# The experts' gate and up products by Strassen's scheme, in a kernel of two transformer layers

## The chip, the cores and the metric

The kernel runs on one core of a Trainium2 chip. The core has TensorE (PE, matrix products; its weight loads are listed apart as PEld), VectorE (DVE), ScalarE (ACT), GpSimd (POOL) and SyncE (SP), which work side by side and wait for each other by semaphores. POOL also issues the indirect DMAs, which gather or scatter rows by an index. The metric is the device time of the whole program in microseconds (us). Seventeen runs of the kernel before gave a median of 1565.16 us, between 1560.81 and 1569.68.

## The reference

Two layers work on 2 x 2048 tokens of width 256, in float32. The part that matters here is the end of the second layer, a mixture of eight experts of which each token takes two. Cut to that, it reads:

```
xf = x.reshape(B * T, D)                       # 4096 x 256
pi = sinkhorn(-(xf @ gate_W.T))                # 4096 x 8
_, top_idx = top_k(pi, 2)
g = einsum('nd,efd->enf', xf, W_gate)          # f: 1024 hidden units
u = einsum('nd,efd->enf', xf, W_up)
y = einsum('enf,edf->end', silu(g) * u, W_down)
out = sum over k of y[top_idx[:, k], n] * pi[:, k]
```

Before it come a gated linear attention with a quantised feed-forward product (layer 0) and an attention of 16 heads with linear biases (layer 1). The change leaves them alone.

## The kernel before

The program has three stages in time: layer 0, the attention of layer 1 (with the routing of the experts beside it), and the experts, which begin at about 840 us of the profiled execution.

The routing sorts the 8192 pairs of token and expert into 32 **blocks** of 256 rows, each with one expert, and two **groups** of four small remainders. `Experts.pieces` (line 2478) goes over the blocks; what it does for one is in `Block`:

- `load` (line 2234) issues two gathers on POOL, `load_gate_up` with 2 MB of gate and up weights and `load_down` with 1 MB of down weights (both line 2209), and on SP the load of the block's rows of the table (`load_places`, line 2225). They are issued at the start of block n for block n + 2.
- `fetch_rows` (line 2239) makes, on DVE, the list of row numbers `to` and the weights `wt` (lines 2244 to 2251), and gathers the 256 rows of normalised tokens into `xb` by two indirect DMAs on POOL (line 2464). It runs in the middle of block n for block n + 2.
- `open_rows` (line 2256) transposes the rows by four products with the identity on PE (line 2265), and ACT copies the 128 x 512 result out of PSUM (line 2270). It runs at the end of block n for block n + 1.
- `hidden` (line 2272) makes the 1024 hidden units in eight slices of 128. A slice has four products of 128 x 128 weights with 256 columns (line 2279): gate and up, each summed over the two halves of the width 256. ACT then takes the silu of the gate (line 2284) and DVE multiplies it by the up product (line 2285). The slices take turns in several PSUM banks.
- `add_rows` (line 2289) multiplies the hidden units of the block before with its down weights: 16 products of 256 columns (line 2308), after the hidden products of the present block. `send` (line 2313) scales the 128 x 256 results on DVE (line 2315) and adds them to the rows of the output by an indirect DMA on POOL (line 2318), one for each of the two tiles of rows. The second one writes to the same tensor as the first, and it is issued only when the first has landed.

A float32 product shows as two records in the profile, each with its own weight load. So the 1024 gate and up products of 32 blocks are 2048 records, and the 512 down products are 1024.

The steps of the two groups (`Group`, from line 2325) are put between blocks: 12 gathers of weights, a gather of rows and four scatters for each group, with their products.

The order on an engine is set in two ways. A framework places each instruction when, by its own plan, its inputs are ready, in the order in which the program names them where several are ready. An instruction that goes through `keep_in_program_order`, or through the small class `InOrder` (line 110) that does this for each call, is put behind the instruction that the program names before it on that engine, whichever that is. At run time each engine works its list strictly in order: an instruction that waits holds back all behind it. In the kernel before, the products, silus and multiplications of the experts are placed freely; the transposes and the small DVE steps of `fetch_rows` are pinned.

The buffers of the experts stage are borrowed from the attention by `rooms` (line 1884): three rooms of gate and up weights, four of down weights, two each for the turned rows and the hidden units. PSUM has six banks for products (tag `mm`) and two for the down products.

Of the kernel before, what the change touches and what calls it, by code (L numbers as in the profile page):

```python
# [1683 lines left out]
def attention(  # L1684
# [198 lines left out]

    def rooms(name, n, shape, dt=F32):
# [12 lines left out]
        if name == "wdown" and n % 4 < 2:  # L1897
            return operands.heads[2][:, n % 4, :]
        if name in ("hT", "wdown"):
            n = n % 2 + (2 if name == "wdown" else 0)  # L1900
            if n not in larger:
                larger[n] = p2.tile([P, 4 * ST], F32, tag="pt", name="larger", bufs=4)
            return larger[n] if n >= 2 else larger[n].rearrange("p (f r) -> p f r", f=NFC)
        if name == "xT":
            t = operands.first_values.rearrange("p t d -> p (t d)")
            return t[:, n % 2 * ST : (n % 2 + 1) * ST].rearrange("p (e r) -> p e r", e=2)
        if name == "sg":
            if name not in larger:
                larger[name] = p2.tile([P, 4, BS], F32, tag="sk_beaten", name="sg", bufs=1)
            return larger[name][:, n % 4, :]  # L1910
        if name == "y":
            t = other_values.rearrange("p t d -> p (t d)")
            return t[:, n % 4 * NC * E : (n % 4 + 1) * NC * E].rearrange("p (c d) -> p c d", c=NC)
# [10 lines left out]
    for n, (pieces, widths, masks, ended) in enumerate(units):  # L1924
# [22 lines left out]
        if routed:  # L1947
            next(sends, None)
            next(decision, None)
        else:  # L1950
            routed = next(background, True) is True
        if n == len(units) - 4:
            ahead[0].open_rows()
# [244 lines left out]
class Block:  # L2198


    def __init__(self, e, n, b):
        self.e, self.n, self.b = e, n, b
        self.tiles, self.rows, self.first = NC, BS, b * BS

# [29 lines left out]
    def load(self):  # L2234
        self.load_gate_up()
        self.load_down()
        self.load_places()
# [17 lines left out]

    def open_rows(self):


        nc, rooms, n, keep = (
            self.e.nc, self.e.rooms, self.tiles, self.e.tc.keep_in_program_order  # L2260
        )
        ps = rooms("x_ps", self.n, [P, 2 * BS]).rearrange("p (e r) -> p e r", e=2)
        for e in range(2):
            for c in range(n):
                keep(nc.tensor.transpose(  # L2265
                    ps[:, e, c * P : (c + 1) * P], self.xb[:, c, e * P : (e + 1) * P],
                    self.e.c.ident,
                ))
        self.xT = rooms("xT", self.n, [P, 2, BS])
        nc.scalar.copy(self.xT[:, :, 0 : self.rows], ps[:, :, 0 : self.rows])  # L2270

    def hidden(self):
        nc, rooms, rows = self.e.nc, self.e.rooms, slice(0, self.rows)
        self.hT = rooms("hT", self.n, [P, NFC, BS])
        for f in range(NFC):
            ps = rooms("h_ps", f, [P, 2 * BS]).rearrange("p (j r) -> p j r", j=2)
            for j in range(2):
                for c in range(2):
                    nc.tensor.matmul(  # L2279
                        ps[:, j, rows], lhsT=self.wgu[:, j, c, f * P : (f + 1) * P],  # L2280
                        rhs=self.xT[:, c, rows], start=c == 0, stop=c == 1,
                    )
            sg = rooms("sg", f, [P, BS])[:, rows]
            nc.scalar.activation(sg, ps[:, 0, rows], AF.Silu)  # L2284
            nc.vector.tensor_tensor(self.hT[:, f, rows], sg, ps[:, 1, rows], ALU.mult)  # L2285
            if f % 2:
                yield

    def add_rows(self, apart=False):

# [4 lines left out]
        else:  # L2295
            ps = self.e.rooms("y_ps", self.n, [P, NC * E]).rearrange("p (c d) -> p c d", c=NC)
            parts = [ps[:, c, :] for c in tiles]
        for c in tiles:
            self.multiply(c, parts[c])
            if apart:  # L2300
                self.send(c, parts[c], y)
        if not apart:
            for c in tiles:
                self.send(c, parts[c], y)

    def multiply(self, c, ps):
        for fc in range(NFC):
            self.e.nc.tensor.matmul(  # L2308
                ps, lhsT=self.hT[:, fc, c * P : (c + 1) * P], rhs=self.wd[:, fc, :],
                start=fc == 0, stop=fc == NFC - 1,  # L2310
# [136 lines left out]
class Experts:  # L2447
# [3 lines left out]
    def __init__(self, tc, a, out, c, rooms, blocks, groups):  # L2451
        self.tc, self.nc, self.a, self.out, self.c = tc, tc.nc, a, out, c
        self.rooms = rooms
# [24 lines left out]
    def pieces(self, begun=False):  # L2478
# [5 lines left out]
        if todo and not begun:  # L2484
            for block in todo[0:2]:
                block.load()
                block.fetch_rows()
            todo[0].open_rows()
        for n, block in enumerate(todo):
# [3 lines left out]
            for part, _ in enumerate(block.hidden()):  # L2493
                if last and part == 0:
                    todo[n - 1].add_rows()
                if part == 1 and n + 2 < len(todo):
                    todo[n + 2].fetch_rows()
                yield
            if not last:
                todo[n + 1].open_rows()  # L2500
            if n and not last:
                todo[n - 1].add_rows()
# [3 lines left out]
        if todo:  # L2506
            todo[-1].add_rows(apart=True)
# [4 lines left out]
def layer1_experts(tc, a, out, c, blocks, groups):  # L2512
    bufs = {"wgateup": 3, "wdown": 4, "xb": 4, "y": 4, "at": 5, "by": 5, "wt": 5, "to": 5,
# [180 lines left out]
```

## Time and profile before

| | |
|---|---|
| median of 17 runs | 1565.16 us |
| the profiled execution | 1564.67 us |
| its span, first to last instruction | 1562.8 us |
| PE busy / PEld busy | 1509.5 us (97%) / 1222.9 us (78%) |
| DVE / ACT / POOL busy | 710.7 (45%) / 641.5 (41%) / 452.0 (29%) us |
| gate and up products, line 2279 | 2048 records, 449.1 us busy |
| down products, line 2308 | 1024 records, 226.6 us busy |
| mean granted clock of TensorE | 0.989 of full speed |

The page gives busy time by engine, the span in 40 slices, the chain of work that ended last, and the costliest groups of instructions by line. Each group has its operands, partitions x elements, the number of records, the busy time and the mean length of one in ns, and the idle time before them with what ended it. The length of a matmul record holds the time that its result needs to come out of the array, so records of a dense row overlap: what one costs is the distance from its start to the next start. The timeline gives starts and lengths, the windows give the busy time of each engine in a stretch, with the granted clock.

### The profile page before, as it was taken

The numbers are of one execution on the slowest core, as the hardware profiler recorded it, in microseconds if no ns is written. First come the engines' busy times: TensorE is split into PE (matmuls) and PEld (weight loads), VectorE is DVE, ScalarE is ACT, GpSimd is POOL, SyncE is SP. The second block draws the span as 40 slices with busy tenths as digits, with TensorE's granted clock in tenths as the row PEclk, the third lists the DMA queues.
The fourth block names the chain that finished last, engine by engine and source line by source line (L and its number), as shares of the span: only waits on it lengthen the run. The fifth ranks groups of instructions, "written<-read, shape, count | busy, mean of one in ns | idle before, by whom it ended". The sixth has DMA issues, their size and how long they took to land.

```text
span 1562.8 us, 32176 instructions
## 1 busy us (share of the span) xinstructions
PE 1509.5 (97%) x13412; PEld 1222.9 (78%) x13412; DVE 710.7 (45%) x2223; ACT 641.5 (41%) x1336; POOL 452.0 (29%) x385
## 2 busy tenths in 40 slices
PE   7889999999999999999999999999999999999996
PEld 4556766766678888788888888888888888888885
DVE  6787767655378876844445222122222221222121
ACT  4444546455467777677774211111111111111110
POOL 4342222112010000771101333333334433343232
PEclk9989999999999999999999999999999999999998
DMA  7001102311460210602305765575856768576521
GB/s 221 0 21 50 56 28 70 75 56 56 118 120 17 46 45 29 105 20 67 114 16 197 224 184 188 181 245 165 286 178 200 221 195 283 166 229 198 184 31 22
DMA packets 75562, 191.59 MB, mean 123 GB/s; under 512 B 18976, under 2 KB 56352, under 8 KB 62944
## 3 DMA queue, kind: packets, MB, share of 16 engines
q0 software_dynamic: 28256, 144.23, 29.2%
q1 hardware_dynamic: 46048, 44.04, 11.3%
q8 instruction: 107, 1.75, 0.5%
q10 hardware_dynamic: 1104, 1.18, 0.2%
q14 instruction: 47, 0.39, 0.1%
HBM read 157.95 MB, written 31.83 MB: 121 GB/s over the span
## 4 chain that ended last, share of the span: by engine, by line
PE 64%; DVE 1%; DMA 0%; issue 0%; POOL 0%; POOLq 0%
PE h_ps L2279 28%; PE y_ps L2308 14%; PE sc L1828 9%; PE o_ps L1848 7%; PE f_ps L1538 1%; PE o_tr L1784 1%; PE x_ps L2265 1%; PE h_ps L2390 1%; PE on_tr L1803 0%; PE h_ps L2425 0%; DVE pt L118 0%; DMA out<-va,to 0%; PE h_ps L2308 0%; PE h_ps L2413 0%; POOL out L2318 0%
## 5 line engine op out<-in xcount | busy, mean ns | idle before, releaser
L2279 PE MATMUL h_ps<-va,qk 128*128 128x256 f32 x2048 | 449.1, 380 | 0.0
L2279 PEld LDWEIGHTS h_ps<-va,qk 128*128 128x128 f32 x2048 | 387.9, 190 | 57.3 <-issue 4.8
L1834 ACT ACTIVATE pt<-sc 128x512 f32<-128x512 f32 (+1 forms) x589 | 302.8, 601 | 103.0 <-ACT pt L1834 42.2
L2284 ACT ACTIVATE sg<-h_ps 128x256 f32<-128x256 f32 x256 | 98.1, 383 | 531.0 <-PE h_ps L2279 531.0
L2285 DVE TENSOR_TENSOR larger<-sg,h_ps 128x256 f32<-128x256 f32 x256 | 107.9, 422 | 329.2 <-ACT sg L2284 329.1
L1828 PE MATMUL sc<-qk 32*128 32x256 f32 (+6 forms) x3544 | 207.6, 333 | 3.4 <-issue 1.5
L1828 PEld LDWEIGHTS sc<-qk 32*128 32x128 f32 x3544 | 176.6, 186 | 32.7 <-issue 17.8
L1848 PE MATMUL o_ps<-pt,va 128*32 128x256 f32 (+7 forms) x3544 | 162.7, 312 | 1.2 <-DVE o_sb L118 1.1
L2318 POOL DMA_INDIRECT out<-va,to x64 | 101.9, 1592 | 172.2 <-issue 73.6
L1848 PEld LDWEIGHTS o_ps<-pt,va 128*32 128x32 f32 x3544 | 126.4, 110 | 26.5 <-issue 6.9
L118 DVE TENSOR_TENSOR pt<-pt,keepmask 128x128 f32<-128x128 f32 (+3 forms) x568 | 121.0, 273 | 36.3 <-ACT pt L1834 35.8
L2177 POOL DMA_INDIRECT table<-rows,place x64 | 63.9, 998 | 200.5 <-DVE pt L118 181.3
L2315 DVE SCALAR_TENSOR_TENSOR va<-y_ps,wt,half_bias 128x256 f32<-128x256 f32 x63 | 27.6, 480 | 203.0 <-PE y_ps L2308 203.0
L2308 PE MATMUL y_ps<-qk,larger 128*128 128x256 f32 x512 | 113.3, 379 | 0.0
L2308 PE MATMUL y_ps<-larger 128*128 128x256 f32 x496 | 109.7, 379 | 0.0
L2308 PEld LDWEIGHTS y_ps<-qk,larger 128*128 128x128 f32 x512 | 96.0, 190 | 12.3
L2308 PEld LDWEIGHTS y_ps<-larger 128*128 128x128 f32 x496 | 93.2, 190 | 12.1
L2464 POOL DMA_INDIRECT xb<-normed,to x64 | 63.6, 994 | 38.6 <-issue 16.8
L2209 POOL DMA_INDIRECT qk<-in_wgateup,wrow x32 | 30.1, 942 | 99.8 <-PE h_ps L2279 55.2
L532 PE MATMUL vf_ps<-qk,xnT 128*128 128x512 f32 x128 | 58.5, 611 | 0.0
L2209 POOL DMA_INDIRECT qk<-in_wdown,wrow x16 | 15.1, 943 | 147.2 <-PE y_ps L2308 72.5
L532 PEld LDWEIGHTS vf_ps<-qk,xnT 128*128 128x128 f32 x128 | 24.3, 195 | 29.1 <-issue 25.6
(281 smaller groups left out, 1791.2 us busy)
## 6 DMA issues: line engine op xcount, KB each, us to landing
qk<-qk SPq DMA_DIRECT2D x32, 256.0 KB
qk<-qk SPq DMA_DIRECT2D x64, 128.0 KB
va<-v SPq DMA_DIRECT2D x4, 1208.0 KB
v<-v SPq DMA_DIRECT2D x8, 574.0 KB
normed<-xn SPq DMA_DIRECT2D x8, 512.0 KB
out<-acc SPq DMA_DIRECT2D x8, 512.0 KB
acc<-in_x SPq DMA_DIRECT2D x7, 512.0 KB
table<-rows,place POOLq DMA_INDIRECT x64, 4.4
```

Source lines behind the costliest of these rows:

```text
L118: return lambda *a, **k: self.tc.keep_in_program_order(begin(*a, **k))
L532: tc.keep_in_program_order(nc.tensor.matmul(*args, **kwargs))
L1828: nc.tensor.matmul(scs[r][:, at : at + q1 - q0], lhsT=heads[rows, 1, kb * P : (kb + 1) * P], rhs=heads[rows, 0, qt * QT + q0 : qt * QT + q ...
L1834: nc.scalar.activation(pt[:, r, 0:width], scs[r][:, 0:width], AF.Exp)
L1848: nc.tensor.matmul(sums[bank][r * HR : (r + 1) * HR, to + q0 : to + q1], lhsT=values[b, way][:, kb, h * VC : h * VC + HR], rhs=pt[:, r, at ...
L2177: send = self.nc.gpsimd.indirect_dma_start(out=self.c.table, in_=self.rows[:, t, :], in_offset=None, out_offset=bass.IndirectOffsetOnAxis( ...
L2279: nc.tensor.matmul(ps[:, j, rows], lhsT=self.wgu[:, j, c, f * P : (f + 1) * P], rhs=self.xT[:, c, rows], start=c == 0, stop=c == 1,)
L2284: nc.scalar.activation(sg, ps[:, 0, rows], AF.Silu)
L2285: nc.vector.tensor_tensor(self.hT[:, f, rows], sg, ps[:, 1, rows], ALU.mult)
L2308: self.e.nc.tensor.matmul(ps, lhsT=self.hT[:, fc, c * P : (c + 1) * P], rhs=self.wd[:, fc, :], start=fc == 0, stop=fc == NFC - 1,)
L2318: nc.gpsimd.indirect_dma_start(out=self.e.out, in_=y[:, c, :], in_offset=None, out_offset=bass.IndirectOffsetOnAxis(ap=self.to[:, c : c + ...
L2464: self.nc.gpsimd.indirect_dma_start(out=to, out_offset=None, in_=self.c.normed, in_offset=bass.IndirectOffsetOnAxis(ap=at, axis=0),)
```

## The change

The gate product G = X Wg and the up product U = X Wu of a block are read as one product of 2 x 2 blocks: the rows of X in two tiles of 128, the width 256 in two halves, and the weights in gate and up. Eight products of such blocks become seven, by Strassen's scheme in Winograd's form, on sums and differences of the operands.

- **`combine`** is new. For half u of the hidden units (512 of them) it makes four sums or differences of weights, each 128 x 512: two on POOL (`s1`, and the room of `up[0]` overwritten) and two on DVE (`s2`, `s4`), all pinned. It is named after each half of block n for the same half of block n + 1, and for block 0 six units before the end of the attention and at the start of the stage.
- **`open_rows`** gets three subtractions on DVE behind the copy, pinned, and moves from the end of block n to the middle of its second half.
- **`hidden`** has, for each half, seven products P1 to P7 of four slices with 128 columns. P1 is copied out of its PSUM tile `w` by ACT, P6 and P7 are added into the same tile and copied out again, P4 is added last and read by DVE. P2 goes to tile `z`, P5 and P3 to tile `v`. DVE adds and multiplies 128 x 512 tiles, ACT takes two silus. Everything is pinned on its engine.
- **`add_rows`** is now a generator of eight pieces of two down products. `hidden` calls four of them in each half: one after P2, one after P5 and two after P7. The eighth piece is followed by the two `send`s.
- **`load_down`** moves from the start of block n to its end (still for block n + 2), with three rooms for down weights in place of four. The `y` rooms go from four to two. Other rooms are laid out anew.

```diff
+        if n == len(units) - 6:
+            ahead[0].combine(0)
         if n == len(units) - 4:
             ahead[0].open_rows()
...
     def load(self):
         self.load_gate_up()
-        self.load_down()
         self.load_places()
...
+    def combine(self, u):
+        e, (gate, up) = self.e, (
+            [self.wgu[:, j, c, u * ST : (u + 1) * ST] for c in range(2)] for j in range(2)
+        )
+        s1, s2, s4 = (e.rooms("combo", 3 * u + n, [P, ST]) for n in range(3))
+        e.gpsimd.tensor_tensor(s1, up[0], up[1], ALU.add)
+        e.gpsimd.tensor_tensor(up[0], gate[0], up[0], ALU.subtract)
+        e.vector.tensor_tensor(s2, s1, gate[0], ALU.subtract)
+        e.vector.tensor_tensor(s4, gate[1], s2, ALU.subtract)
+        self.factors[u] = (gate[0], gate[1], s4, up[1], s1, s2, up[0])
+
     def open_rows(self):
...
+        for i, (k, c) in enumerate(((0, 0), (0, 1), (1, 1), (1, 0))):
+            e.tensor.transpose(ps[:, i, :], self.xb[:, c, k * P : (k + 1) * P], e.c.ident)
+        x = e.rooms("xT", self.n, [P, 4, P])
+        e.scalar.copy(x, ps)
+        t, s = (e.rooms("xt", 2 * self.n + i, [P, 2, P]) for i in range(2))
+        vector.tensor_tensor(t, x[:, 1:3, :], x[:, 0:2, :], ALU.subtract)
+        vector.tensor_tensor(s[:, 0, :], x[:, 2, :], t[:, 0, :], ALU.subtract)
+        vector.tensor_tensor(s[:, 1, :], x[:, 3, :], s[:, 0, :], ALU.subtract)
...
+            def product(n, ps, first=False, last=False):
+                for f in range(4):
+                    e.tensor.matmul(
+                        ps[:, f, :], lhsT=self.factors[u][n - 1][:, f * P : (f + 1) * P],
+                        rhs=self.turned[n - 1], start=first and f == 0, stop=last and f == 3, skip_group_check=True,
                     )
...
+            sg = e.rooms("sg", u, [P, 2, 4, P])
+            one, two = (self.hT[:, 4 * u : 4 * u + 4, c * P : (c + 1) * P] for c in range(2))
+            product(1, w, first=True)
+            e.scalar.copy(sg[:, 0], w)
+            product(2, z, first=True, last=True)
+            e.vector.tensor_tensor(sg[:, 0], sg[:, 0], z, ALU.add)
+            next(others, None)
+            product(6, w)
+            e.scalar.copy(sg[:, 1], w)
+            e.scalar.activation(sg[:, 0], sg[:, 0], AF.Silu)
+            product(5, v, first=True)
+            next(others, None)
+            product(7, w)
+            e.scalar.copy(two, w)
+            e.vector.tensor_tensor(two, two, v, ALU.add)
+            yield
+            next(others, None)
+            next(others, None)
+            product(4, w, last=True)
+            e.vector.tensor_tensor(one, sg[:, 0], w, ALU.mult)
+            product(3, v, last=True)
+            e.vector.tensor_tensor(sg[:, 1], sg[:, 1], v, ALU.add)
+            e.scalar.activation(sg[:, 1], sg[:, 1], AF.Silu)
+            e.vector.tensor_tensor(two, two, sg[:, 1], ALU.mult)
+            yield
...
+        for half in range(2):
+            for c in tiles:
+                for n in (4 * half, 4 * half + 2):
+                    self.multiply(c, parts[c], range(n, n + 2), c == 0, c > 0)
+                    if n < NFC - 2 or c < NC - 1:
+                        yield
         for c in tiles:
-            self.multiply(c, parts[c])
...
+            self.send(c, parts[c], y)
+        yield
...
+        self.tensor, self.vector, self.scalar, self.gpsimd = (
+            InOrder(tc, engine) for engine in (self.nc.tensor, self.nc.vector, self.nc.scalar, self.nc.gpsimd)
+        )
...
         for n, block in enumerate(todo):
             if n + 2 < len(todo):
                 todo[n + 2].load()
             last = n + 1 == len(todo)
-            for part, _ in enumerate(block.hidden()):
-                if last and part == 0:
-                    todo[n - 1].add_rows()
+            others = todo[n - 1].add_rows() if n else iter(())
+            for part, _ in enumerate(block.hidden(others)):
                 if part == 1 and n + 2 < len(todo):
                     todo[n + 2].fetch_rows()
+                if part % 2 and not last:
+                    todo[n + 1].combine(part // 2)
+                if part == 2 and not last:
+                    todo[n + 1].open_rows()
                 yield
-            if not last:
-                todo[n + 1].open_rows()
-            if n and not last:
-                todo[n - 1].add_rows()
+            if n + 2 < len(todo):
+                todo[n + 2].load_down()
             while between and between[0][0] <= n and not last:
                 between.popleft()[1]()
```

## The prediction

> **What bounds the kernel now.** I began with the page. PE is busy almost throughout, and the chain that ended last is PE's own, led by the line that the change replaces.
>
> ```profile
> PE 1509.5 (97%) x13412; PEld 1222.9 (78%) x13412; DVE 710.7 (45%) x2223; ACT 641.5 (41%) x1336; POOL 452.0 (29%) x385
> ...
> L2279 PE MATMUL h_ps<-va,qk 128*128 128x256 f32 x2048 | 449.1, 380 | 0.0
> ```
>
> Then the windows of the experts stage (columns: window, length, busy us and records of PE, PEld, DVE, ACT and POOL, granted clock, DMA share, GB/s). PE has no gap; the others are a quarter to a third busy. While this holds, PE's records are the time.
>
> ```profile
> 900.00:1180.00 280.00, 280.00 (x1356) 241.70 (x1355) 61.49 (x177) 48.95 (x120) 99.43 (x86) 1.00 0.63 201
> ```
>
> Next the timeline of PE, for the distance from one record to the next (columns: start, length, engine, line, tiles, count). 13 records of 256 columns last 2.97 us; less the last one's 0.379, over 12, that is 0.216 us each. 16 records of 128 columns with 128 x 128 weights, in layer 0, last 1.95; less 0.275, over 15, 0.1117 us. Half the columns cost 0.52, not 0.50.
>
> ```profile
> 1060.72 2.97 PE L2279 MATMUL h_ps<-va,qk 128*128 128x256 f32 x13
> ```
> ```profile
> 24.09 1.95 PE L532 MATMUL c_ps<-qk,soft 128*128 128x128 f32 x16
> ```
>
> Last POOL's timeline. The gather of down weights waits for PE's last down product, so its starts give the period of a block: 1078.65 - 1057.49 = 21.16 us. The second scatter (L2318) starts 5.95 us after the first.
>
> ```profile
> 1057.49 0.94 POOL L2209 DMA_INDIRECT qk<-in_wdown,wrow  x1 [6.40 <-PE y_ps L2308]
> 1058.74 1.61 POOL L2318 DMA_INDIRECT out<-va,to  x1 [0.30 <-issue]
> 1064.69 1.58 POOL L2318 DMA_INDIRECT out<-va,to  x1 [4.34 <-issue]
> 1066.58 1.01 POOL L2464 DMA_INDIRECT xb<-normed,to  x1 [0.30 <-issue]
> 1067.89 0.99 POOL L2464 DMA_INDIRECT xb<-normed,to  x1 [0.30 <-issue]
> ...
> 1078.65 0.94 POOL L2209 DMA_INDIRECT qk<-in_wdown,wrow  x1 [6.41 <-PE y_ps L2308]
> ```
> ```profile
> 1523.21 1.56 POOL L2318 DMA_INDIRECT out<-va,to  x1 [11.28 <-DVE va L2315]
> 1527.75 1.55 POOL L2318 DMA_INDIRECT out<-va,to  x1 [2.97 <-DMA out<-va,to]
> ```
>
> With no gather of weights just ahead it is 4.54 us: issue 1.56, landing 2.97.
>
> **PE's own work.** A block has 64 records of gate and up, 32 of down (0.216 each: 13.81 + 6.91) and 4 transposes of 0.11 (0.44): 21.16, the period seen. After, 2 halves x 7 products x 4 slices x 2 = 112 records of 0.1117 are 12.51; with down and transposes 19.86. That is 1.30 less per block, 41.6 over 32.
>
> The Trainium skill, "TensorE: Matmul & The Clock Gate", section "The mechanism", speaks against the change: a weight load overlaps running matmuls only in other row groups, and by "LDWEIGHTS" it takes columns / 1.2 GHz, 107 ns. By that estimate, load and product one after the other, the 3584 records would cost about 0.214 each and the change 325 us. The row of 128 columns above contradicts it.
>
> **The new waits.** All is now pinned on its engine, and two chains run beside PE. Their prices are rows of the same size:
>
> ```profile
> L118 DVE TENSOR_TENSOR acc<-acc,f_ps 128x512 f32<-128x512 f32 x32 | 22.0, 687 | 26.7 <-PE f_ps L1538 25.9 <-PE sk_ps L1538 0.8
> L2315 DVE SCALAR_TENSOR_TENSOR va<-y_ps,wt,half_bias 128x256 f32<-128x256 f32 x63 | 27.6, 480 | 203.0 <-PE y_ps L2308 203.0
> L219 POOL TENSOR_TENSOR mx_r<-mx_r,mx_pw 128x512 f32<-128x512 f32 x17 | 21.6, 1272 | 83.9 <-DVE mx_r L218 57.7 <-DVE arg L719 23.6 <-DVE ln_veo L144 2.5
> L2270 ACT COPY va<-x_ps 128x512 f32<-128x512 f32 x32 | 18.8, 586 | 4.5 <-PE x_ps L2265 2.9
> L1834 ACT ACTIVATE pt<-sc 128x512 f32<-128x512 f32 x579 | 299.3, 604 | 98.2 <-ACT pt L1834 41.0 <-issue 30.8 <-PE sc L1828 24.7
> ```
>
> So a large DVE step is 0.69 (0.69 from SBUF alone too, L201), a POOL sum 1.27, a copy 0.59, a silu 0.60 (Exp's row), a product of P1 to P7 0.89, a piece 0.86. A result leaves PE 0.2 after its last slot; a hand-off between other engines takes 0.03 to 0.08, taken as 0.05.
>
> P4 adds into `w`, so it waits for the copy of P7. ACT makes that copy behind the first silu, which waits for DVE's addition of P2. DVE makes that behind `s4` and `s2` of the `combine` named before it, and `s2` waits for POOL's `s1`. So PE's P4 hangs on POOL.
>
> Chain A, from P4 of a block's first half to P4 of its second: P4 and P3 1.79, out of PE 0.2, `sg1` addition 0.69, silu 0.60, multiplication 0.69, `to` 0.17 (L2244), two gathers of `xb` 2.6 (`s1` is pinned behind them), `s1` 1.27, `s2` and `s4` 1.38, addition 0.69, silu 0.60, copy 0.59, six hand-offs 0.3: 11.6 us. PE's work in the same stretch is seven products, four pieces, the transposes: 10.15. PE waits 1.4.
>
> Chain B, from there to P4 of the next block's first half. The eighth piece ends as P4 starts, but its `send` is behind the opened rows on DVE: copy 0.59, three subtractions 1.01 (L118 rows of 256 and 128 columns: 0.43, 0.29, 0.29), `send` 0.48, first scatter to second 4.54, second scatter and its gap 1.88, `s1` 1.27 (pinned behind it), `s2` and `s4` 1.38, addition 0.69, silu 0.60, copy 0.59, hand-offs 0.3: 13.3 us. PE's work is seven products and four pieces, 9.71. It waits 3.6, part of it at P6, whose copy is behind the previous silu on ACT.
>
> The period is 24.9 us where it was 21.16. Thirty blocks have both chains.
>
> **The price of `s2` beside POOL.** `up[0]` runs on POOL as `s1` ends, beside `s2` and `s4`. Bounds: 0 (DVE's 0.69 unchanged) and 1.27 (the whole of it) per chain. In the nearest row, a DVE step with two SBUF inputs began 0.20 us after a POOL step and took 1419 ns, not 693:
>
> ```profile
> L210 DVE SCALAR_TENSOR_TENSOR mx_r<-mx_pw,mx_v x16: 658/693/1419, 34.7 to 356.1; 128x512 f32<-128x512 f32 x16
> ```
>
> I take its 0.73, twice per block: period 26.3, or 5.2 more than before; 30 x 5.2 = 156.
>
> **The clock.** Where PE was busy 1.31 of 3.42 us (a gap of 2.57 in it), the granted clock was 0.50 in the next window:
>
> ```profile
> 97.13:100.55 3.42, 1.31 (x12) 1.12 (x11) 3.42 (x12) 0.79 (x2) 2.35 (x1) 1.00 0.00 0
> 100.55:103.96 3.41, 2.95 (x8) 2.12 (x9) 2.88 (x11) 1.10 (x3) 1.11 (x2) 0.50 0.00 0
> ```
>
> The wait before P4 is of that size, once per block. Half clock for 3.4 us costs PE 1.7, of which only P4 and P3 are on chain A: 0 to 1.8 per block. I take 1.0, as the rest falls into PE's spare time: 30.
>
> The Trainium skill, "TensorE: Matmul & The Clock Gate", section "Why this matters for your kernels", allows gaps of up to about 3 us; by it this term would be nearer 0. The row's gap of 2.57 already halved the clock.
>
> **The rest.** The groups' POOL work (24 gathers of 1.25, eight scatters of 4.5) now delays sums, while 25 us of their products (L2390, L2425, L2413, L2377) fill PE's waits: between 0 and 30, taken as 10, since their gathers fit into POOL's free time and only the scatters exceed it. Block 0 has no pieces to cover its copies, and the last has no sums to wait for: -3 to 8, taken as 3. `combine` for block 0 in the attention: nothing, as POOL idles there for 67 us (768 to 836) and its weights were asked for at 739; without that cover 4 us once. `load_down` later: nothing, since its weights are used two blocks on; one period if that failed. SP's table load stays where it was, and nothing new is queued behind it. PSUM: three tiles per half in six banks, read long before their turn comes again: nothing, or 0.7 per half if a bank were late. DVE (11 us of work per block) and ACT (6.6) are not bounds.
>
> **The sum.** 1564.67 + 156 (in which PE's saving is included) + 30 + 10 + 3 = 1763.7 us against the profiled execution, whose time is 0.5 below the median.
>
> **Rivals.** (1) The chains hide, and PE stays the bound: 1564.67 - 41.6 = 1523. For it: PE has no gap now, and DVE and ACT would be at most 55% busy. It decides if the two chains together take less than 21.16, 5.2 less than I have; the wait for the first scatter (4.5) and the gathers ahead of `s1` (2.6) would have to fall out. Against it: the scatter's wait stands in the trace before.
> (2) The scatters don't hold `s1` (the order on POOL turns out otherwise), chain A alone binds: 11.6 + 9.7 + 0.7 = 22.0, 1564.67 + 30 x 0.84 + 13 = 1603 at most, 1569 without the price beside POOL and the 13 of the rest.
> (3) A weight load costs its recorded 190 ns, not its distance: 3584 x 0.190 = 681 in place of 442, 1804. Against: 16 records in 1.95 us.
> (4) All bounds at their upper end, with a weight gather ahead of the first scatter (5.95, not 4.54): 5.2 + 1.1 + 1.8 + 1.4 = 9.5 per block, 1564.67 + 285 + 38 = 1888.
>
> **Chances.** The two chains, 1603 to 1825: 70%. Rival 1: 10%. Rival 2: 11%, of which 2% within 0.2%, about what a measurement here can tell from no change. Rivals 3 and 4, 9% together, half below 1825. The range reaches from 1600 to 1825 and leaves out about 2 in 10: rival 1, most of rival 2, the upper end of rival 4. So faster 10%, same 2%, slower 88%.
>
> **What would show it.** Right: L2279's successor at 0.112 per record, PE with two waits per block, the longer before P4 of the first half, released by ACT; `s2` released by POOL, POOL's sums right behind the second scatter; a period near 26; the clock at 0.5 in places. Wrong: PE busy 100% with a period of 19.9, or `s1` ahead of the scatters on POOL. The weakest steps are the price beside POOL, the clock, and the order of POOL's list, which I take from the pins in the code.

## The result and the profile after

The changed kernel takes 1763.58 us (median of 8 runs, 1762.21 to 1766.29) where the kernel before takes 1564.87 (47 runs): a ratio of 1.1276, 95% interval 1.1264 to 1.1289. It is 199 us slower, and 1763.7 was forecast. The profiled execution has a span of 1759.2 us.

First the page of the kernel after. Every operation that is now pinned on its engine is recorded at line 118, so the groups are told apart by their tiles.

```profile
PE 1537.7 (87%) x14948; PEld 1282.9 (73%) x14948; DVE 994.8 (57%) x2511; ACT 721.8 (41%) x1400; POOL 646.8 (37%) x513
...
L118 PE MATMUL h_ps<-va,qk 128*128 128x128 f32 x1024 | 149.4, 300 | 75.1 <-ACT larger L118 75.0
```

PE's busy share fell from 97% to 87%, and the groups of gate and up products, which had no idle time ahead of them before, now wait for ACT. The same window of the experts stage as before (length, then busy us and records of PE, PEld, DVE, ACT and POOL, granted clock, DMA share, GB/s) says how much:

```profile
900.00:1180.00 280.00, 230.13 (x1563) 206.94 (x1563) 137.97 (x233) 64.26 (x115) 140.06 (x108) 0.93 0.49 155
```

PE rests for 50 of 280 us where it rested for none, at a mean granted clock of 0.93 in place of 1.00. DVE and POOL, the next, are busy for half of it: no engine is the bound by its own work. Such a picture calls for the waits, here those of the kernel after by engine (who waited for whom: us in total, times, longest):

```profile
ACT larger L118 <- DVE larger L118: 263.8, 55, 12.3
...
PE h_ps L118 <- ACT larger L118: 156.0, 51, 9.8
DVE larger L118 <- POOL larger L118: 121.7, 26, 11.7
DVE va L118 <- POOL va L118: 102.7, 26, 10.3
...
POOL out L2376 <- DMA out<-va,to: 34.3, 17, 3.8
```

Read from the second line outwards, this is the chain of the prediction: PE's P4 waits for ACT's copy, ACT's silu for DVE's addition, DVE's `s2` for POOL's `s1`, and POOL, ahead of `s1`, for the landing of the first scatter. DVE's two waits for POOL go by tile: `va` holds the first half's sums, `larger` the second half's. PE's timeline shows one such wait (start, length, engine, line, tiles, count, idle time before):

```profile
1046.07 2.07 PE L118 MATMUL h_ps<-second,qk 128*128 128x128 f32 x8 [3.65 <-ACT larger L118]
1047.94 1.92 PE L118 MATMUL h_ps<-larger,bidx 128*128 128x128 f32 x8
...
1060.04 1.16 PE L118 MATMUL h_ps<-second,qk 128*128 128x128 f32 x8 [0.64 <-ACT larger L118]
1061.03 1.06 PE L118 MATMUL h_ps<-larger 128*128 128x128 f32 x8
...
1075.74 1.95 PE L118 MATMUL h_ps<-va,qk 128*128 128x128 f32 x16
```

At 1046.07 P4 of a first half has waited 3.65 us, and it and P3 then take 2.07 and 1.92 us where the second half's take 1.16 and 1.06: the clock is halved just where it counts. The last line is the pace at full clock: 16 records in 1.95 us less one record's own tail, 0.112 us each, as in layer 0 before.

POOL's timeline has the order on which the chain hangs:

```profile
1030.48 0.96 POOL L2229 DMA_INDIRECT larger<-in_wdown,wrow  x1 [0.76 <-PE y_ps L118]
1034.39 1.63 POOL L2376 DMA_INDIRECT out<-va,to  x1 [2.95 <-DVE va L2373]
1036.32 0.98 POOL L2229 DMA_INDIRECT qk<-in_wgateup,wrow  x1 [0.30 <-PE h_ps L118]
1039.00 1.59 POOL L2376 DMA_INDIRECT out<-va,to  x1 [1.70 <-DMA out<-va,to]
1040.05 1.85 POOL L118 TENSOR_TENSOR larger<-qk 128x512 f32<-128x512 f32 x1
1041.97 1.77 POOL L118 TENSOR_TENSOR qk<-qk 128x512 f32<-128x512 f32 x1
...
1055.93 1.78 POOL L118 TENSOR_TENSOR qk<-qk 128x512 f32<-128x512 f32 x1
...
1294.39 1.59 POOL L2494 DMA_INDIRECT out<-group_y,group_to  x1 [2.24 <-DMA out<-va,to]
...
1298.40 1.59 POOL L2494 DMA_INDIRECT out<-group_y,group_to  x1 [0.73 <-DMA out<-group_y,group_to]
...
1305.68 1.63 POOL L2494 DMA_INDIRECT out<-group_y,group_to  x1 [0.30 <-issue]
...
1311.17 1.59 POOL L2494 DMA_INDIRECT out<-group_y,group_to  x1 [1.43 <-DMA out<-group_y,group_to]
...
1316.72 1.60 POOL L2376 DMA_INDIRECT out<-va,to  x1 [2.68 <-DMA out<-group_y,group_to]
```

The second scatter waits for the first (4.61 us from start to start), and `s1` and `up[0]` stand directly behind it. In two blocks the four scatters of a group stand on POOL's list too, 4.0 to 7.3 us from one to the next, and three of the five waits shown end with the landing of a group's scatter; those blocks last 36.6 and 37.6 us. The other 28 between the first block and the last have a mean period of 27.36 us.

DVE's timeline beside POOL's step at 1055.93 shows the price of two engines side by side: `s2` takes 0.69 us, and `s4` 1.64.

```profile
1055.88 0.69 DVE L118 TENSOR_TENSOR va<-va,qk 128x512 f32<-128x512 f32 x1 [3.56 <-POOL va L118]
1056.61 1.64 DVE L118 TENSOR_TENSOR bidx<-qk,va 128x512 f32<-128x512 f32 x1
```

### The profile page after: what moved, and what is told of

Its sections match the earlier page's. It is cut to its first block, busy times and chain, and to the rows that moved or that the text cites. A ratio compares the mean times of both kernels' runs of the same rounds, so it can differ in the third digit from the quotient of the medians.

```text
span 1759.2 us, 35864 instructions
## 1 busy us (share of the span) xinstructions
PE 1537.7 (87%) x14948; PEld 1282.9 (73%) x14948; DVE 994.8 (57%) x2511; ACT 721.8 (41%) x1400; POOL 646.8 (37%) x513
## 3 DMA queue, kind: packets, MB, share of 16 engines
q1 hardware_dynamic: 46048, 44.04, 10.1%
## 5 line engine op out<-in xcount | busy, mean ns | idle before, releaser
L118 PE MATMUL h_ps<-va,qk 128*128 128x128 f32 x1024 | 149.4, 300 | 75.1 <-ACT larger L118 75.0
L118 PEld LDWEIGHTS h_ps<-va,qk 128*128 128x128 f32 x1024 | 140.8, 213 | 90.0 <-ACT larger L118 85.4
L118 DVE TENSOR_TENSOR larger<-larger,h_ps 128x512 f32<-128x512 f32 x160 | 109.8, 686 | 154.4 <-ACT larger L118 91.5
L118 PE MATMUL y_ps<-qk,larger 128*128 128x256 f32 x688 | 169.5, 380 | 0.0
L118 ACT ACTIVATE larger<-larger 128x512 f32<-128x512 f32 x64 | 40.3, 630 | 263.8 <-DVE larger L118 263.8
L118 ACT ACTIVATE va<-va 128x512 f32<-128x512 f32 x64 | 40.3, 630 | 259.1 <-DVE va L118 259.0
L118 PE MATMUL h_ps<-second,qk 128*128 128x128 f32 x256 | 44.6, 328 | 80.4 <-ACT larger L118 80.4
L118 ACT COPY larger<-h_ps 128x512 f32<-128x512 f32 x128 | 73.6, 575 | 90.0 <-PE h_ps L118 89.9
L118 POOL TENSOR_TENSOR qk<-qk 128x512 f32<-128x512 f32 x64 | 107.2, 1685 | 4.1
L118 PEld LDWEIGHTS h_ps<-second,qk 128*128 128x128 f32 x256 | 38.7, 228 | 90.8 <-ACT larger L118 90.5
```

The costliest lines, as they stand in the source:

```text
L118: return lambda *a, **k: self.tc.keep_in_program_order(begin(*a, **k))
```

## The experiments

My theory was that two chains through POOL set the end: A, from P4 of a block's first half to P4 of its second, through the gathers of `xb` and the first half's sums; and B, from there to P4 of the next block's first half, through both scatters and the second half's sums. The rivals were that PE's own records had become dearer, that one of the chains alone was the cause, or that the price of two engines beside each other was.

The table has all runs. A and B are medians in us, read between the copies that release P4; rests and half clock are sums in us over the experts stage, worked out from the trace's records. A rest is counted from the end of a record's slot, so that it comes out somewhat longer than the idle time of the views (163 us by these for the kernel after, 9 with all sums on DVE). The second half's, the first half's, `up[0]` from `s2`, the first run of all sums on DVE and the first half's with `s2` were timed once each. On three chips used later every kernel traced there, and by its times the kernel before, spends some 85 us more in the attention stage, in a stretch in which PE rests for the most part (with all sums on DVE 28 of the 87 us from 630 to 717 are busy, at a clock of 0.50; in the kernel after 85 are); its cause is open, so a difference is always taken to the kernel before on the same chip.

| kernel | time | before there | difference | A | B | PE's rests | half clock |
|---|---|---|---|---|---|---|---|
| after | 1763.6 | 1564.9 | +198.7 | 13.4 | 14.0 | 174 | 159 |
| both halves' sums early | 1566.3 | 1562.9 | +3.4 | 9.7 | 10.1 | 30 | 33 |
| second half's early | 1655.0 | 1562.9 | +92.1 | 13.0 | 10.3 | 103 | 85 |
| first half's early | 1781.4 | 1562.9 | +218.5 | 11.3 | 18.5 | 195 | 233 |
| `up[0]` from `s2` | 1700.8 | 1562.9 | +137.9 | 12.1 | 13.1 | 132 | 113 |
| both early, `send` pinned | 1635.9 | 1649.4 | -13.5 | 9.7 | 10.1 | 20 | 24 |
| all sums on DVE | 1625.6 | 1649.4 | -23.8 | 9.8 | 10.1 | 11 | 21 |
| first early, second's `up[0]` from `s2` | 1828.8 | 1649.4 | +179.4 | 10.8 | 17.1 | 167 | 193 |
| repeats into P2's bank | 1873.7 | 1647.7 | +226.0 | 13.8 to 15.7 | 14.1 | 113 | 71 |
| all sums on DVE, again | 1623.1 | 1647.7 | -24.7 | | | 11 | |
| all on DVE, `send` pinned | 1622.5 | 1647.7 | -25.2 | | | 11 | |
| repeats into a spare bank | 1825.9 | 1651.4 | +174.5 | 12.3 | 14.0 | 106 | 71 |

### Both sums ahead of the gathers and scatters

```diff
+                if part % 2 == 0 and part // 2 in (0, 1) and not last:
+                    todo[n + 1].add_weights(part // 2)
                 if part == 1 and n + 2 < len(todo):
                     todo[n + 2].fetch_rows()
```

`add_weights` holds the two POOL steps of `combine`, which keeps `s2` and `s4` on DVE. The work is the same; its place on POOL differs.

> POOL's two steps of combine are named in the first part of each half, ahead of the gathers of xb and of the two scatters; the DVE steps stay where they are. The two chains (mine): s2 no longer waits for POOL, chain A shrinks to about 9.3 us of DVE and ACT work, under PE's 10.15, chain B to about 10 against PE's 9.71; period near 20.3 in place of 27.3, time 1530 to 1570. Rival, records of 128 columns and strict order on DVE and ACT are the cost: nothing moves, 1750 or more. Rival, POOL's sums are the cost wherever they stand, by their contention with DVE: at most 2 us per block less, 1700 or more.

Measured: 1566.27 us (10 runs), a ratio of 1.002 (1.0007 to 1.0032). The same window as above, of this kernel:

```profile
900.00:1180.00 280.00, 274.19 (x2042) 257.11 (x2041) 155.53 (x305) 85.51 (x152) 180.48 (x142) 0.99 0.62 204
```

PE executes 2042 records there where the kernel after executes 1563, and POOL is busy for 180 us where it is for 140 there, so neither PE's records nor POOL's amount of work cost the 199 us: the place of the two steps of each half on POOL's list cost them. The time is in the range that the theory gave, at its upper end. An undisturbed block takes 19.85 us, PE's own work. Part of what keeps the kernel from being faster is a third wait. In some blocks with a group's steps, the DVE step of `send` (L2381), which isn't pinned, came to stand between `s2` and `s4` and waited for PE's eighth piece:

```profile
1025.87 0.68 DVE L118 TENSOR_TENSOR va<-va,qk 128x512 f32<-128x512 f32 x1
1031.87 0.48 DVE L2381 SCALAR_TENSOR_TENSOR va<-y_ps,wt,half_bias 128x256 f32<-128x256 f32 x1 [5.32 <-PE y_ps L118]
1032.27 0.68 DVE L118 TENSOR_TENSOR bidx<-qk,va 128x512 f32<-128x512 f32 x1
```

PE then rests for 2.9 us. That happened four times, and behind two of the rests the clock fell. A fifth rest, of 5.2 us at 1232.09, has another reason: there two scatters of a block, behind those of a group, stand ahead of `s1` on POOL's list, and `s2` waits for `s1` for 7.9 us.

### The same, with `send` pinned

```diff
-        nc.vector.scalar_tensor_tensor(
+        self.e.vector.scalar_tensor_tensor(
             y[:, c, :], ps, self.wt[:, c : c + 1], self.e.c.half_bias, ALU.mult, ALU.add
```

> As both_early, with the DVE step of send pinned in its place. In both_early the blocks without a group's steps took 19.85 us, and 13 gaps of PE, 29.8 us in all, lie in others: at five of them, 3.07 us each, the framework had put the first send, which waits for PE's eighth piece, ahead of s4 on DVE. Mine: these five gaps and the half clock behind them go, 1535 to 1555, faster than the kernel before by 0.5 to 1.8%. Rival: the gathers of the groups' weights on POOL hold s1 back in those blocks, whatever DVE's order is: within 5 of 1566.

Measured: 1635.88 us against 1649.42, a ratio of 0.991 (0.9894 to 0.9925), in the range expected; the absolute time can't be compared, as that chip was one of the longer attention. The four rests are gone, not five as I had counted; the fifth, behind a group's scatters, is still there, with 4.4 us. There it was POOL's list, as the rival had it, though by scatters and not by the gathers of the groups' weights.

### One half at a time

Two kernels with `in (1,)` and `in (0,)` in place of `in (0, 1)` above.

> The same for the second half only, so that s1 and up[0] of the second half stand ahead of the scatters; the first half stays behind the gathers of xb. The two chains: chain B falls from 14.0 to PE's 9.7 to 10, chain A stays at 13 to 14; period 23 to 24, time 1630 to 1665. Rival (records and strict order): 1750 or more.

> The same for the first half only, ahead of the gathers of xb; the second half stays behind the scatters. The two chains: chain A falls from 13 to 14 to PE's 10.2 to 10.6, chain B stays at 14.0; period 24.3, time 1655 to 1690. Rival (records and strict order): 1750 or more.

The second half's sums early gave 1655.0, in the range: 107 us less than the kernel after, by the differences in the table. Chain B gives most of it, while A stays at 13.0: with `s1` no longer behind the second scatter, B is 3.7 us shorter. The first half's sums early gave 1781.4, 20 more than the kernel after by the differences, where a gain of 75 to 110 was expected: a miss. Chain A fell to 11.3, but B grew to 18.5. POOL's timeline of that kernel, over one block:

```profile
1040.85 0.94 POOL L2229 DMA_INDIRECT larger<-in_wdown,wrow  x1 [4.14 <-PE y_ps L118]
1042.10 1.63 POOL L2384 DMA_INDIRECT out<-va,to  x1 [0.30 <-issue]
1044.03 1.30 POOL L2229 DMA_INDIRECT qk<-in_wgateup,wrow  x1 [0.30 <-issue]
1048.22 1.59 POOL L2384 DMA_INDIRECT out<-va,to  x1 [2.89 <-DMA out<-va,to]
1049.27 1.83 POOL L118 TENSOR_TENSOR larger<-qk 128x512 f32<-128x512 f32 x1
1050.49 1.82 POOL L118 TENSOR_TENSOR va<-qk 128x512 f32<-128x512 f32 x1
1051.71 3.03 POOL L118 TENSOR_TENSOR qk<-qk 128x512 f32<-128x512 f32 x2
```

And DVE's, at the end of it:

```profile
1051.14 4.16 DVE L118 TENSOR_TENSOR larger<-larger,qk 128x512 f32<-128x512 f32 x1 [6.67 <-POOL larger L118]
1055.34 0.69 DVE L118 TENSOR_TENSOR larger<-qk,larger 128x512 f32<-128x512 f32 x1
```

Two things differ from the kernel after. All four sums now stand in a row behind the second scatter, the `larger` of one block and the `va` of the next, and `s2` beside them takes 4.16 us in place of 0.69: it ends 0.56 us after the last of the row. And the gather of down weights stands 1.25 us ahead of the first scatter instead of 3.91, and from scatter to scatter it is 6.12 us instead of 4.61. These are 3.5 and 1.5 us on chain B. The gather, issued just ahead of the first scatter, moves that by 0.7 as well (3.03 us from the start of DVE's addition behind the release to the scatter, 2.35 in the kernel after), and `s4` falls back from 1.64 to 0.69: 4.7 in all in this block, where B's median grew by 4.5. In all blocks of this kernel with the gather 1.25 ahead the median from scatter to scatter is 6.07 us, so this block is an ordinary one.

> As first_early, which took 1781 (I had expected 1655 to 1690): there POOL's four sums ran one behind the other after the second scatter, and s2, ready after the first of them, took 4.16 us. Here up[0] of the second half is made from s2, so that POOL has no step to run beside s2. If POOL's train held s2 back: s2 0.69, chain B 13 to 13.5, chain A at PE's 9.7 to 10.2, 1640 to 1680. Rival, s2 was long for another reason: 1750 to 1790.

That kernel adds the edit of the next section to the second half alone. It gave 179.4 more than the kernel before of its chip, 39 less than the first half alone: a miss again, by some 65 us, and nearer to what the rival had (185 to 225 more). `s2` fell from 4.16 to 1.74 and `s4` rose to 1.63, as the row on POOL goes on beside them, and from scatter to scatter it was 7.05 us in the block looked at (1006.98 to 1014.03), with the gather of down weights 1.25 ahead; the median of the 23 such blocks is 6.02, where the kernel after has 4.67. So I had named one of two causes; the second was not tested by a run of its own.

### The price of two engines side by side

`up[0]` can be had as `up[1] - s2`, since `s2` is `up[0] + up[1] - gate[0]`. It then waits for `s2` and starts beside `s4` only.

```diff
-        e.gpsimd.tensor_tensor(up[0], gate[0], up[0], ALU.subtract)
         e.vector.tensor_tensor(s2, s1, gate[0], ALU.subtract)
+        e.gpsimd.tensor_tensor(up[0], up[1], s2, ALU.subtract)
         e.vector.tensor_tensor(s4, gate[1], s2, ALU.subtract)
```

> up[0] is made as up[1] minus s2, the same value, so that POOL's second step waits for s2 and no longer runs as s4 begins; nothing else moves. If s2 and s4 are held back beside POOL's step (my price 0.73 per chain; the changed kernel shows s4 at 1.64 in place of 0.69): s4 near 0.69, both chains about 0.95 shorter, period near 25.4, time 1690 to 1715. Rival, no such price, s4 is long for another reason: time within 5 of 1763.

Measured: 1700.82 us, in the range. DVE's timeline, and POOL's beside it:

```profile
1038.51 0.69 DVE L118 TENSOR_TENSOR va<-va,qk 128x512 f32<-128x512 f32 x1 [3.56 <-POOL va L118]
1039.24 0.69 DVE L118 TENSOR_TENSOR bidx<-qk,va 128x512 f32<-128x512 f32 x1
```
```profile
1037.20 1.27 POOL L118 TENSOR_TENSOR va<-qk 128x512 f32<-128x512 f32 x1
1039.28 1.78 POOL L118 TENSOR_TENSOR qk<-qk,va 128x512 f32<-128x512 f32 x1 [0.81 <-DVE va L118]
```

`s4` is now first by 0.04 us, takes 0.69, and POOL's step pays. Both chains are shorter by 0.9 (B's median 13.1, A's shortest blocks 11.3 against 12.2 at full clock), and the time by 61 us (198.7 less 137.9), of which 30 blocks of 1.8 make 54; the rest may be the clock (half clock 113 us in place of 159).

### All four sums on DVE

```diff
-        e.gpsimd.tensor_tensor(s1, up[0], up[1], ALU.add)
-        e.gpsimd.tensor_tensor(up[0], gate[0], up[0], ALU.subtract)
+        e.vector.tensor_tensor(s1, up[0], up[1], ALU.add)
+        e.vector.tensor_tensor(up[0], gate[0], up[0], ALU.subtract)
```

> The changed kernel with all four steps of combine on DVE, so that nothing of them waits for POOL or stands beside it. Mine: four steps of 0.69 add 2.76 to each chain's DVE work, chain A 9.4 and chain B 10.2 by my rows; period 20 to 21, 1550 to 1605. Rival, DVE's work in strict order is the cost and not the wait for POOL: DVE has 2.8 us more to do per block, 1763 or more.

> The kernel with all four sums of a half on DVE a second time, in enough rounds for an interval. By the theory PE is the bound again and only the starting blocks wait: 1541 us on a chip where the kernel before has 1564.9, a ratio of 0.983 to 0.988. If the earlier gain of 1.4% belonged to that one chip, with its longer attention, the ratio is 0.99 or above.

> All four sums on DVE and the step of send held in its place on DVE as well. With the sums early on POOL, that pin took away five waits of 3.1 us. With the sums on DVE no such wait is left in the trace, so the theory expects the same time as without the pin, within 2 us. The rival: the unpinned step is held in front of s4 here too, and the pin gives 5 to 15 us more.

Measured: 1625.62 against 1649.42, and, on another chip, 1623.05 against 1647.7, a ratio of 0.985 (0.9837 to 0.9864), in the range given for the second run. The first had been expected at 1550 to 1605 on a chip with the shorter attention; 23.8 us less than the kernel before is 1541 there, faster than that range. With the pinned `send` it was 1622.51, 0.9844 (0.983 to 0.9857), the same. DVE's timeline, from the run that was timed five times over, has the four sums one behind the other, 2.7 us in all. The window of the same execution, taken 85 us later in the span because the attention is longer there, has PE without a gap:

```profile
1049.01 0.68 DVE L118 TENSOR_TENSOR va<-qk 128x512 f32<-128x512 f32 x1
1049.73 0.69 DVE L118 TENSOR_TENSOR qk<-qk 128x512 f32<-128x512 f32 x1
1050.34 0.68 DVE L118 TENSOR_TENSOR va<-va,qk 128x512 f32<-128x512 f32 x1
1051.06 0.69 DVE L118 TENSOR_TENSOR bidx<-qk,va 128x512 f32<-128x512 f32 x1
```
```profile
985.00:1265.00 280.00, 280.00 (x2115) 262.62 (x2118) 191.37 (x367) 86.56 (x155) 115.60 (x91) 1.00 0.64 207
```

This version beats both kernels. It keeps 24.7 of the 41.6 us that the change takes from PE's records. What is missing is 17 us. Rests of 11 us at the start of the stage and 21 us of half clock at its two ends, of which up to half is lost (the kernel before has 8 us of it too), are of that size; no run tested it.

### Useless products in PE's waits

To measure the clock by itself, PE was given work that nobody reads, in the time in which it waits anyway.

```diff
+            for _ in range(1 if u else 3):
+                product(1, z, first=True, last=True)
             product(4, w, last=True)
```

> The changed kernel with repeated products in PE's waits: ahead of P4, the product P1 is made again into the bank of P2, which DVE has read by then (three times in a block's first half, once in its second; 0.89 us each at full clock, 3.6 us a block, nobody reads them). The changed kernel's PE waits about 4.2 us ahead of the first half's P4 and 2 us ahead of the second half's. Theory (the chains set the end, and the half clock that follows PE's waits lengthens P4 and P3, which are on the chains): the repeats lie in the waits, the granted clock stays at 1.0 or nearly, and the time falls by 0.9 to 1.4 us in each of 30 blocks: 27 to 42 us, 1720 to 1740 where the changed kernel has 1764. Rival A (the half clock costs only work that the chains hide): within 8 us of the changed kernel. Rival B (PE's own work, not the chains, sets the end): later by 3.6 us a block, 110 us.

Measured: 1873.71 against 1647.7, 27 us more than the kernel after costs. None of the three was met, and the reason is in PE's timeline: the repeats go to the bank that DVE adds from behind `s4`, and so they begin only when the wait is nearly over.

```profile
1202.14 2.94 PE L118 MATMUL h_ps<-larger,qk 128*128 128x128 f32 x24 [1.75 <-DVE larger L118]
1204.92 1.06 PE L118 MATMUL h_ps<-second,qk 128*128 128x128 f32 x8
```

The copy that P4 needs had ended at 1203.22. Half clock fell to 71 us from 159, but the repeats stood on the chain. The second try writes to the bank of the block's transposes, which was read long ago, and only in a first half:

```diff
+        self.spare = ps
...
+            if not u and self.n:
+                for _ in range(3):
+                    product(1, self.spare, first=True, last=True)
             product(4, w, last=True)
```

> The repeated products again, so placed that they can begin as PE's wait begins: only in a block's first half, ahead of P4, P1 three times into the bank of the block's own transposes, which ACT has copied long before (2.68 us of PE work at full clock in a wait of about 3.65; in the run before, the repeats went to P2's bank and waited for DVE's addition from it, behind s2 and s4, and so began only 1.1 us ahead of P4's release). Theory: PE's longest rest in a block falls to about 1 us, the half clock behind it goes, P4 and P3 take 0.9 us each in place of up to 1.8 each, and the time falls by 0.9 to 1.4 us in each of 30 blocks: against the kernel before on the same chip +157 to +172 us where the changed kernel has +199, a ratio near 1.10 on a chip where the kernel before has 1648. Rival A (the half clock costs nothing, the chains do not feel it): +190 to +207. Rival B (the repeats begin late here too): above +207.

Measured: 1825.91 against 1651.39, +174.5 where the kernel after has +198.7; outside the range that the theory gave by 2.5 us, though its interval (a ratio of 1.1022 to 1.1079, 169 to 178 us) reaches into that range, and below the other two. The kernel with 2.7 us more work in a block is 24 us faster, each against the kernel before on its chip. PE's timeline over one block:

```profile
1180.63 2.84 PE L118 MATMUL x_ps<-larger,qk 128*128 128x128 f32 x24
1183.46 1.16 PE L118 MATMUL h_ps<-second,qk 128*128 128x128 f32 x8
...
1195.70 1.16 PE L118 MATMUL h_ps<-second,qk 128*128 128x128 f32 x8 [1.83 <-ACT larger L118]
...
1209.81 1.16 PE L118 MATMUL h_ps<-va,qk 128*128 128x128 f32 x8 [1.07 <-ACT larger L118]
```

No rest of this block is above 1.9 us and P4 takes 1.16 each time. With the clock out of the way the two chains can be read off: 12.24 and 14.11 us. The median block is 26.31 where the kernel after has 27.33, so filling the wait gained 1.0 us in a block. It did not end the half clock: 71 us of it are left, some of them behind the second halves' rests of 1.8 us.

## Why the prediction was right, step by step

**PE's own work.** 19.86 us per block was forecast; blocks whose sums come in time take 19.85 (both sums early, and all on DVE).

**Weight loads.** Rival 3 had 0.190 us for a record; they run at 0.112, and with all sums on DVE, where PE is the bound, the time is below the one before. The rule of the Trainium skill that was weighed in the prediction ("TensorE: Matmul & The Clock Gate", section "The mechanism"), that a load overlaps only with products in other row groups, is contradicted by this row again; the same section also lets a load into a background weight buffer run ahead, which would agree with the row.

**Chain A.** 11.6 and 0.73 were forecast, 12.3; 12.24 was measured at full clock. By its parts, from the timelines of the kernel with the spare bank: P4 to the gathers 4.51 (4.3 forecast), gathers 2.27 (2.6), `s1` 1.27 (1.27), `s2` and `s4` up to the next addition 2.33 (2.16), from there to P4 1.86 (2.0). It was the stretch that rival 2 wanted alone; with the second half's sums early, the kernel nearest to it, the time is +92 where rival 2 had +38 at most: its shortest blocks take 22.3 us, near the 22.0 of rival 2, but its median block 23.6, and the clock falls there too.

**Chain B.** 13.3 and 0.73 were forecast, 14.0; 14.0 was measured (14.11 in the block shown). P4 to the first scatter 2.33 (2.2), scatter to scatter 4.71 (4.54), second scatter to the end of `s1` 2.88 (1.88 and 1.27), `s2` and `s4` 2.32 (2.16), to P4 1.87 (2.0). The second scatter lets POOL go after 1.04 us instead of 1.88, but `s1` beside its tail takes 1.84 us instead of 1.27; the two errors cancel for the most part.

**The price beside POOL.** 0.73 taken, 0.95 measured (`s4` 1.64 for 0.69), and 0.9 per chain when it was taken away. It fell on `s4`, where the text had `s2`. I had it from a row with one step on each side; in the kernel with the first half's sums early, where POOL's sums stand in a row, the price was 3.5 us.

**The clock.** 30 us taken; filling the wait gained 24, 18 of them in the thirty blocks. That is not the whole price: half clock fell from 159 us to 71 and not to nothing, and in some blocks the repeats themselves cost time (the longest block grew from 37.6 to 40.6 us).

**The rest.** The sum had 156, 30 and 10 for thirty blocks, 196 us. From the release of P4 in the second block to that in the last they take 840.3 us; before, thirty periods of 21.16 and the 25 us of the groups' products make 659.8. So they cost 180 us more. The two blocks with a group's scatters take 9 to 10 us each over the mean, some 20 where 10 was taken, but the 25 us of the groups' products, which the sum left in its base, now lie mostly in PE's waits: the groups cost about nothing. For the first and the last block and the ends of the stage 3 was taken, with 8 as the upper bound. Of the 196.5 us between the two profiled executions some 16 lie there. The kernel with all sums on DVE spends within 1 us the same there (36.1 us from the first product to the first of these releases and 37.0 behind the last; 37.1 and 37.8 in the kernel after), so POOL's sums are not the reason; what is was not traced.

So the mechanism was right and the sum was met, 1763.7 against a median of 1763.58, but that it was met to 0.2 us is luck: the two chains and the clock came out about as worked out, and some 10 us too much for the groups stand against some 13 too little for the two ends.

**The rivals.** The first, PE as the bound, was 10% likely and needed the scatter and the gathers to fall out of the chains. That is what the early sums do, and PE is then the bound; its own saving of 41.6 us was still not reached by any version, for what lies at the two ends of the stage. The fourth had a weight gather ahead of the first scatter; in the kernel after it is 3.9 us ahead and does no harm, in the kernels with the first half early 1.25, where it goes with 1.4 us more from scatter to scatter.

## What to carry to other kernels

An engine's list is a queue for everything on it: before a step that the critical engine needs is put on an engine that also issues scatters, read from the trace what stands ahead of it and for how long it waits there; sums behind gathers and scatters cost 199 us here, the same sums ahead of them 3, and on another engine the change gained 25. Work out a loop as chains between two fixed points, with every hand-off a measured row; in each stretch the longer of the chain and of PE's own work sets the pace, whatever the busy shares say. When a critical step follows a wait of PE, look at the granted clock behind it before looking for another cause.

## What the runs showed of the hardware that I had not expected

With the first half's sums early, a DVE step with two SBUF inputs beside a row of POOL steps was held until the whole row had ended: 4.16 us for 0.69 beside three steps. In the kernel after it took 1.64 beside one that had begun 0.68 earlier; where DVE's step was first, by 0.04 us, it took 0.69 and POOL's 1.78 in place of 1.27. The Trainium skill, "SBUF — State Buffer", section "SBUF: two separate sides", says that the two engines share a pair of ports as an exclusive lock, held for a whole instruction by whoever starts first, and names a DVE operation with two SBUF inputs against a GpSimd operation that reads SBUF. The runs agree for a single step on each side. In a row it came out both ways: the wait of 4.16 us lasted for all three steps, but with the second half's `up[0]` made from `s2`, `s2` (1.74 us from 1016.95) was held by one step and ended 0.56 us behind it, and only `s4` by the next. What decides between the two is not shown.

From scatter to scatter, with the second waiting for the first to land, the time went with how far ahead a gather of down weights had been issued. Over all runs here, 207 pairs with the gather 1.24 to 1.33 us ahead took 5.6 to 10.2 us, median 6.0, and 65 pairs with it 3.5 to 4.5 ahead 4.5 to 5.8, median 4.66; from 1.8 to 2.9 ahead there is anything from 4.5 to 7.4. The kernel with the spare bank has both: 5.83 in four blocks and 4.64 in 24. No run changed this distance alone, so it is a pattern and not a test.

How long PE rested did not settle whether half clock followed. A rest of 2.91 us in the kernel with both sums early was followed by it twice (P3 in 1.92 us) and twice not, and the rest of 2.57 us on which the prediction's clock term rests recurs in the kernel after (at 101 us) without it. The first line below is from the kernel after, a rest of 3.70 us with P4 at full clock behind it; the other two, from the kernel with the spare bank, show a rest of 1.84 us and P3 at half clock. Of 24 rests of 1.8 to 1.9 us in that kernel five were followed by half clock. It came in stretches of 3.41 us or whole multiples of it, but for the last at the end of the program.

```profile
1019.80 1.16 PE L118 MATMUL h_ps<-va,qk 128*128 128x128 f32 x8 [3.70 <-ACT larger L118]
```
```profile
1062.24 1.36 PE L118 MATMUL h_ps<-va,qk 128*128 128x128 f32 x8 [1.84 <-ACT larger L118]
1063.39 1.92 PE L118 MATMUL h_ps<-va,larger 128*128 128x128 f32 x8
```

And 2.7 us of products that nobody reads, put into a wait, made a kernel 24 us faster.
